# Two convolution outputs from three products instead of four, with operands laid out by phase of the token index

## The chip, the cores and the metric

One core of one Trainium2 chip runs the whole program. The metric is the device time of one execution in microseconds; the kernel before takes 2332 us.

Engine names are the profile's: PE is TensorE's matmuls, PEld its weight loads, DVE VectorE, ACT ScalarE, POOL GpSimd, SP the queue that issues most DMAs.

## The reference, cut to what matters

A layer over 32 graphs of 512 nodes with 256 channels: layer norm and ReLU, then three things that feed a gated unit: a dense graph kernel (with a mask), gates, and a convolution of 17 taps along the tokens. All is fp32.

```python
h = relu(bn1(conv1d(xc, conv1_w, 0)))        # 256 -> 256, one tap
h = bn2(conv1d(h, conv2_w, 8))               # 256 -> 256, 17 taps, padding 8
x_conv = relu(h + xc)
A = exp(-dist) * mask                        # 512 x 512 for each graph
x_nmp = A @ relu(x @ w_msg.T + b_msg)
x_in = concat(x_conv, x_nmp)
# r, z, n from x_in @ w_ih.T and x @ w_hh.T; out = (1 - z) * n + z * x
```

## The kernel before

The 17 taps (padded to 18 = 3 x 3 x 2) are done by a fast algorithm of two levels: at each level three outputs from five products, so 25 products for a group of four batches, with the last factor of two done directly. The code is shortened. A product `m` has weights `w` [2 taps, 2 x 128 input channels, 256] and a moving operand `x2`. Eight such groups give 200 products.

```python
G = 4; U = 57                      # batches a group, blocks of 9 tokens
NU = G * U                         # 228 columns a matmul
cps, acc, gps, tr = ...            # four PSUM pools, two banks each: eight banks
...
w, x2 = WS[m], X2[m].rearrange("p (r v) -> p r v", v=V)
ps = cps.tile([P, N], F32, name="ps_c")[:, :NZ]
for o in range(ND):                                  # ND = 2 halves of the channels
    matmul_sum(ps[:, o * NU : (o + 1) * NU],
        [(w[:, k, i, o * P : (o + 1) * P], x2[:, i * G : (i + 1) * G, k : k + U])
         for k in range(2) for i in range(ND)])      # 2 x 4 matmuls of 228 columns
    yield 1.71                                       # PE time, for the schedule
```

A scheduler in Python writes one instruction list for each engine and mixes several streams in it (convolution, gates, graphs, rows, output); each `yield` gives the PE time of a step. The order of a list is fixed when the program is written. Weights and operands are made ahead:

```python
AHEAD, AHEAD_W = 4, 2
w = cv.tile([P, 2, ND, D], F32, name="w", bufs=3)    # 512 KB, fetched two products ahead
nc.sync.dma_start(w, WD[n])
```

And three users of the transpose pool `tr` (two banks):

```python
def norm_t(b, d):        # input halves d = 0, 1: four transposes, then ACT's ReLU reads them
def factors_t(lane):     # graph factors: one transpose, ACT copies it; four more, ACT copies them
def finish(b, o_sb, c):  # output halves c = 0, 2: four transposes, DVE adds them to the residual
```

## Time and profile before

| | before |
|---|---|
| time | 2332 us |
| PE busy, start-up to 210 us | 133 of 210 us |
| PE busy, convolution 210 to 2153 us | 1919 of 1943 us |
| mean granted TensorE clock | 0.978 |

The lines behind this table stand in the prediction. One line is added here. Columns: stretch in us, its length, then busy time and instructions of PE, PEld, DVE, ACT and POOL, granted clock, DMA share, GB/s.

```profile
210.00:2153.00 1943.00, 1918.91 (x6928) 1231.52 (x6927) 1118.80 (x1741) 541.29 (x758) 312.89 (x185) 1.00 0.43 126
```

In the convolution's stretch PE waits 24 us in all and the clock is full. So the kernel is bound by PE's instruction stream.

### The profile page before, as it was taken

How to read it: one execution, taken by the hardware profiler on the slowest of the kernel's cores; microseconds unless marked ns; L12 is line 12 of the kernel's file. 1: busy time of each engine (PE TensorE's matmuls, PEld its weight loads, DVE VectorE, ACT ScalarE, POOL GpSimd, SP SyncE). 2: the span in 40 equal slices, each digit the busy share in tenths (PEclk: the TensorE clock that was granted, in tenths of full speed). 3: DMA queues.
4: the chain of work that ended last, by engine and by line, in shares of the span. 5: the costliest groups of instructions: out<-in, count | busy, mean ns of one | idle time of the engine just before them, and what ended most of it. 6: DMA issues, size and time to landing. Idle time of an engine off the chain costs nothing.

```text
span 2329.1 us, 21478 instructions
## 1 busy us (share of the span) xinstructions
PE 2212.5 (95%) x7712; PEld 1374.2 (59%) x7712; DVE 1292.6 (56%) x2117; ACT 651.7 (28%) x936; POOL 367.0 (16%) x242
## 2 busy tenths in 40 slices
PE   4768898999999999999999999999999999999998
PEld 2335775665666666666566666656666666666443
DVE  5875766665555655656455655655455535464211
ACT  2442224332324222322224222242313111311211
POOL 1000000111110111122021212212111212222222
PEclk8878999999999999999999999999999999999999
DMA  6665654545444434444434454434333233232121
GB/s 199 180 193 153 181 184 126 149 122 157 144 117 118 126 115 139 136 126 128 112 107 129 131 145 132 113 108 113 135 102 117 82 118 108 100 115 93 63 72 37
DMA packets 388219, 292.58 MB, mean 126 GB/s; under 512 B 280720, under 2 KB 330256, under 8 KB 387472
## 3 DMA queue, kind: packets, MB, share of 16 engines
q1 hardware_dynamic: 370688, 244.53, 37.2%
q10 hardware_dynamic: 17424, 46.67, 5.2%
q8 instruction: 61, 1.00, 0.2%
q14 instruction: 46, 0.38, 0.0%
HBM read 227.69 MB, written 63.44 MB: 125 GB/s over the span
## 4 chain that ended last, share of the span: by engine, by line
PE 87%; DVE 5%; DMA 4%; ACT 2%; issue 1%; POOL 0%; SPq 0%; ACTq 0%; POOLq 0%; DVEq 0%
PE ps_acc L687 42%; PE ps_c L93 24%; PE ps_g L93 8%; PE ps_g L588 8%; PE ps_tr L602 1%; PE ps_g L571 1%; PE ps_tr L254 1%; DMA hd<-hT 1%; PE ps_acc L588 1%; DVE ps_tr L581 1%; DMA w<-wd 1%; PE ps_tr L559 1%; DMA m_sb<-in_adj_dram 1%; DMA nd<-xnmp 1%; ACT w L369 0%
## 5 line engine op out<-in xcount | busy, mean ns | idle before, releaser
L93 PEld LDWEIGHTS ps_c<-x,w 128*128 128x128 f32 x3200 | 602.0, 190 | 142.3 <-issue 120.5
L93 PE MATMUL ps_c<-x,w 128*128 128x228 f32 x3200 | 671.5, 357 | 10.3 <-DMA w<-wd 6.7
L687 PE MATMUL ps_acc<-xconv,wih 128*128 128x512 f32 x768 | 362.1, 594 | 6.2 <-ACT xconv L698 6.2
L687 PE MATMUL ps_acc<-hTb,whh 128*128 128x512 f32 x768 | 357.5, 595 | 4.5 <-DMA hTb<-hd 4.1
L687 PE MATMUL ps_acc<-xnb,wih 128*128 128x512 f32 x768 | 361.2, 593 | 0.0
L724 POOL TENSOR_TENSOR o_sb<-hTb,r 128x512 f32<-128x512 f32 x64 | 101.3, 1583 | 1454.4 <-ACT r L719 1253.3
L718 DVE TENSOR_TENSOR r<-ps_acc,r 128x512 f32<-128x512 f32 x64 | 44.3, 692 | 374.4 <-PE ps_acc L687 374.4
L687 PEld LDWEIGHTS ps_acc<-hTb,whh 128*128 128x128 f32 x768 | 144.9, 190 | 149.3 <-issue 141.6
L687 PEld LDWEIGHTS ps_acc<-xnb,wih 128*128 128x128 f32 x768 | 144.6, 189 | 145.6 <-issue 144.5
L687 PEld LDWEIGHTS ps_acc<-xconv,wih 128*128 128x128 f32 x768 | 143.2, 190 | 144.6 <-issue 132.2
L588 PE MATMUL ps_g<-at,msg 128*128 128x512 f32 x464 | 215.2, 608 | 7.0 <-DVE at L582 7.0
L278 DVE SCALAR_TENSOR_TENSOR x<-x,x 128x471 f32<-128x471 f32 (+1 forms) x184 | 172.8, 939 | 2.6
L275 DVE TENSOR_TENSOR x<-x 128x471 f32<-128x471 f32 x200 | 171.1, 872 | 0.1
L709 DVE SCALAR_TENSOR_TENSOR r<-ps_acc,vec,r 128x512 f32<-128x512 f32 x64 | 48.1, 751 | 220.8 <-PE ps_acc L687 198.8
L588 PEld LDWEIGHTS ps_g<-at,msg 128*128 128x128 f32 x464 | 89.8, 195 | 112.9 <-issue 95.4
L535 DVE TENSOR_TENSOR msg<-ps_g,bmsg 128x256 f32<-128x256 f32 x116 | 48.9, 422 | 170.6 <-PE ps_g L93 170.2
L93 PE MATMUL ps_g<-wmsg,hT 128*128 128x259 f32 x464 | 120.6, 398 | 15.5 <-DVE aug L536 7.8
L715 ACT ACTIVATE z<-ps_acc,brz 128x512 f32<-128x512 f32 x64 | 44.1, 688 | 308.1 <-PE ps_acc L687 300.2
L93 PEld LDWEIGHTS ps_g<-wmsg,hT 128*128 128x128 f32 x464 | 87.7, 196 | 56.2 <-issue 35.9
L725 POOL TENSOR_TENSOR o_sb<-z,o_sb 128x512 f32<-128x512 f32 x64 | 118.1, 1845 | 5.0
L719 ACT ACTIVATE r<-r,vec 128x512 f32<-128x512 f32 x64 | 46.3, 724 | 254.7 <-DVE r L718 254.7
L147 POOL TENSOR_TENSOR rstd<-veps,mhalf 128x4 f32<-128x4 f32 x32 | 37.9, 1184 | 488.2 <-DVE veps L146 488.0
(109 smaller groups left out, 2122.8 us busy)
## 6 DMA issues: line engine op xcount, KB each, us to landing
w<-wd SPq DMA_DIRECT2D x200, 512.0 KB, 3.8
m_sb<-in_adj_dram SPq DMA_DIRECT2D x512, 64.0 KB, 2.4
hd<-hT ACTq DMA_DIRECT2D x32, 512.0 KB, 5.3
nd<-xnmp ACTq DMA_DIRECT2D x64, 256.0 KB, 2.0
hTb<-hd SPq DMA_DIRECT2D x32, 512.0 KB, 4.6
xnb<-nd SPq DMA_DIRECT2D x64, 256.0 KB, 2.8
res<-in_x_dram SPq DMA_DIRECT2D x64, 256.0 KB, 4.0
out_dram<-res SPq DMA_DIRECT2D x64, 256.0 KB, 2.4
```

The lines of the kernel that those rows point to most:

```text
L93: nc.tensor.matmul(ps, lhsT, rhs, start=(i == 0), stop=(i == len(pairs) - 1))
L275: nc.vector.tensor_tensor(dst, get(a), get(b), op=ALU.subtract)
L278: nc.vector.scalar_tensor_tensor(dst, a, -2.0, b, op0=ALU.mult, op1=ALU.add)
L535: nc.vector.tensor_tensor(msg[:, c, :], ps[:, :D], bmsg[:, :D], op=ALU.add)
L588: nc.tensor.matmul(ps, msg[:, c, d * P : (d + 1) * P], at[:, c, :], start=(c == 0), stop=(c == NT - 1))
L687: nc.tensor.matmul(ps, w[:, at + i, cols(o, g)], hT[:, i, :] if k == 0 else x_in[2 * k - 2 + i], start=(k == of[0] and i == 0), stop=(k == ...
L709: nc.vector.scalar_tensor_tensor(r, ps_h, vec[:, _COL["b_hh"] + 2 * ND + o : _COL["b_hh"] + 2 * ND + o + 1], r, op0=ALU.add, op1=ALU.mult,)
L715: nc.scalar.activation(z, ps_z, AF.Sigmoid, bias=brz[:, ND + o : ND + o + 1])
L718: nc.vector.tensor_tensor(r, ps_n, r, op=ALU.add)
L719: nc.scalar.activation(r, r, AF.Tanh, bias=vec[:, _COL["b_ih"] + 2 * ND + o : _COL["b_ih"] + 2 * ND + o + 1],)
L724: nc.gpsimd.tensor_tensor(t, hT[:, o, :], r, op=ALU.subtract)
L725: nc.gpsimd.tensor_tensor(t, z, t, op=ALU.mult)
```

## The change

Two outputs of a two-tap filter need four products directly. With `d0 w0 + d1 w1` and `d1 w0 + d2 w1` they come from three: `(d0 - d1) w0`, `(d2 - d1) w1` and the shared middle `d1 (w0 + w1)`. A block has 18 tokens instead of 9, so a matmul has 4 x 29 = 116 columns: 12 matmuls of 116 columns a product for 8 of 228, 24% fewer columns. For this the operand is laid out by phases of the token index. The core of the diff, with cuts and with comments added:

```diff
-U = 57
+U = 29
+Q = 18
...
+    bps = ctx.enter_context(tc.tile_pool(name="bps", bufs=1, space=PSUM))
-    tr = ctx.enter_context(tc.tile_pool(name="tr", bufs=2, space=PSUM))
+    tr = ctx.enter_context(tc.tile_pool(name="tr", bufs=1, space=PSUM))
...
+    def ends(x2):                      # both differences, on POOL
+        xd = cv.tile([P, 2, RV], F32, name="xd", bufs=2)
+        nc.gpsimd.tensor_tensor(xd, d02, x2[:, 1:2, :].to_broadcast([P, 2, RV]), op=ALU.subtract)
...
-                w = cv.tile([P, 2, ND, D], F32, name="w", bufs=3)
+                w = cv.tile([P, 3, ND, D], F32, name="w", bufs=2)
+                nc.gpsimd.tensor_tensor(w[:, 2], w[:, 0], w[:, 1], op=ALU.add)   # start-up only
...
-    AHEAD, AHEAD_W = 4, 2
+    AHEAD, AHEAD_W = 3, 1
...
+                while len(XD) < min(m + 2, len(X2)):
+                    XD.append(ends(X2[len(XD)]))
+                ps = bps.tile([P, N], F32, name="ps_b")[:, :NH]
+                product(ps, 2, x2)
+                mid = cv.tile([P, NH], F32, name="mid", bufs=2)
+                nc.scalar.activation(mid, ps, AF.Copy)
+                yield 0.88
+                ps = cps.tile([P, N], F32, name="ps_c")[:, :NZ]
+                for k in range(2):
+                    product(ps[:, k * NH : (k + 1) * NH], k, xd[:, k])
+                yield 1.76
...
     def kernel_exp(lane, at):          # four exponentials of a graph
-            pss += [lane.ps(), tr.tile([P, N], F32, name="ps_tr")]
+            lane.ps(), tr.tile([P, N], F32, name="ps_tr"),
+            lane.ps(), bps.tile([P, N], F32, name="ps_b"),
     def masked(lane, b, at, c):
-        ps = tr.tile([P, N], F32, name="ps_tr")
+        ps = lane.ps()
```

So the saving in columns is paid with depth: one bank instead of two for transposes, two buffers instead of three for weights that are half as large again, and two new things a product waits for (its differences and the middle bank). Two smaller cuts: operands are made three products ahead instead of four, and the graphs' messages are sent from the tile `right` of the graph factors instead of a tile of their own.

More of the change, by code (lines that the diff above doesn't have):

```diff
@@ L32 @@
 G = 4
-U = 57
-V = U + 2
-ROW = 9 * V
+U = 29
+V = U + 1
+Q = 18
+LEAD = 9
 ORDER = (3, 0, 4, 2, 1)
@@ L77 @@
     NU = G * U
-    NZ = ND * NU
+    NH = ND * NU
+    NZ = 2 * NH
+    RV = NR * V
     const = ctx.enter_context(tc.tile_pool(name="const", bufs=1))
@@ L126 @@
     wraw = prep.tile([P, ND, 2, 3, 3, D], F32)
-    nc.gpsimd.memset(wraw[:, :, 1, 2, 2, :], 0.0)
+    nc.gpsimd.memset(wraw[:, :, 0, 0, 0, :], 0.0)
     wflat = wraw.rearrange("p i a b c o -> p i (a b c) o")
@@ L160, in bn_affine @@
         return sc, sh
-    h1 = const.tile([P, NR, ROW], F32)
-    nc.gpsimd.memset(h1[:, :, :PAD], 0.0)
-    nc.gpsimd.memset(h1[:, :, PAD + N :], 0.0)
+    h1 = const.tile([P, Q, NR, V], F32)
+    for q, v in ((slice(0, LEAD), slice(0, 1)), (slice(Q - 1, Q), slice(V - 2, V - 1)), (slice(0, Q), slice(V - 1, V))):
+        nc.gpsimd.memset(h1[:, q, :, v], 0.0)
     class Lane:
@@ L263, in conv1 @@
         matmul_sum(ps, [(w1[:, i, o * P : (o + 1) * P], hT[:, i, :]) for i in range(ND)])
-        nc.scalar.activation(
-            h1[:, o * G + b % G, PAD : PAD + N], ps, AF.Relu,
-            bias=bn1_sh[:, o : o + 1], scale=bn1_sc[:, o : o + 1],
-        )
-    def fives(get, new, n):
-        def sub(dst, a, b):
-            nc.vector.tensor_tensor(dst, get(a), get(b), op=ALU.subtract)
+        r, h = o * G + b % G, V - 2
+        blocks = ps[:, : Q * h].rearrange("p (v q) -> p q v", q=Q)
@@ new lines, in conv1, with fives, get @@
+        for dst, src in (
+            (h1[:, LEAD:, r, :h], blocks[:, :LEAD, :]),
+            (h1[:, :LEAD, r, 1 : h + 1], blocks[:, LEAD:, :]),
+            (h1[:, LEAD : LEAD + N - Q * h, r, h], ps[:, Q * h :]),
+        ):
+            nc.scalar.activation(
+                dst, src, AF.Relu, bias=bn1_sh[:, o : o + 1], scale=bn1_sc[:, o : o + 1],
+            )
+    def fives(src, n, new):
+        flat = src.rearrange("p q e -> p (q e)")
+        def get(k, some=n):
+            return src[:, k : k + 3 * some - 2 : 3, :]
+        def sub(dst, a, b):
+            some = n if a < 3 else n - 1
+            nc.vector.tensor_tensor(dst[:, :some, :], get(a, some), get(b, some), op=ALU.subtract)
+            if a > 2:
+                at = [src[:, 3 * n - 3 + b, :], flat[:, (b - 3) * RV + 1 : (b - 2) * RV + 1]]
+                nc.vector.tensor_tensor(
+                    dst[:, some, :], flat[:, (a - 3) * RV + 1 : (a - 2) * RV + 1], at[b > 2],
+                    op=ALU.subtract,
+                )
@@ L277, in less2 @@
         def less2(dst, a, b):
             nc.vector.scalar_tensor_tensor(dst, a, -2.0, b, op0=ALU.mult, op1=ALU.add)
+        size = n * RV
         d1 = new()
-        sub(d1[:, :n], 3, 1)
-        yield d1, n
+        sub(d1, 3, 1)
+        yield d1, size
         for a, b in ((2, 0), (4, 2)):
             t = new()
-            sub(t[:, :n], a, b)
-            yield None, n
+            sub(t, a, b)
+            yield None, size
             if b == 0:
-                less2(t[:, :n], t[:, :n], d1[:, :n])
+                less2(t, t, d1)
@@ L289, in fives @@
             else:
-                less2(t[:, :n], d1[:, :n], t[:, :n])
-            yield t, n
+                less2(t, d1, t)
+            yield t, size
         f2 = new()
-        sub(f2[:, :n], 3, 2)
-        yield None, n
+        sub(f2, 3, 2)
+        yield None, size
         t = new()
-        sub(t[:, :n], 2, 1)
-        yield None, n
-        less2(t[:, :n], t[:, :n], f2[:, :n])
-        yield t, n
-        less2(f2[:, :n], get(1), f2[:, :n])
-        yield f2, n
-    N1, N2 = NR * ROW // 3 - 1, NR * V - 1
+        sub(t, 2, 1)
@@ L305, in operands @@
+        yield None, size
+        less2(t, t, f2)
+        yield t, size
+        less2(f2, get(1), f2)
+        yield f2, size
     def operands():
-        h1f = h1.rearrange("p r t -> p (r t)")
         for x1, size in fives(
-            lambda k: h1f[:, k : k + 3 * N1 - 2 : 3],
-            lambda: cv.tile([P, NR * ROW // 3], F32, name="x1", bufs=3),
-            N1,
+            h1.rearrange("p q r v -> p q (r v)"), 6,
+            lambda: cv.tile([P, 6, RV], F32, name="x1", bufs=3),
         ):
@@ L313, in operands @@
             yield None, size
-            if x1 is None:
-                continue
-            yield from fives(
-                lambda k: x1[:, k : k + 3 * N2 - 2 : 3],
-                lambda: cv.tile([P, NR * V], F32, name="x2", bufs=7),
-                N2,
-            )
-    WD = [dram.tile([P, 2, ND, D], F32, name=f"wd{n}") for n in range(25)]
+            if x1 is not None:
+                yield from fives(x1, 2, lambda: cv.tile([P, 2, RV], F32, name="x2", bufs=6))
+    def ends(x2):
+        xd = cv.tile([P, 2, RV], F32, name="xd", bufs=2)
+        d0 = x2[:, 0, :]
+        d02 = bass.AP(d0.tensor, d0.offset, [d0.ap[0], (1, 2), (1, RV)])
+        nc.gpsimd.tensor_tensor(
+            xd, d02, x2[:, 1:2, :].to_broadcast([P, 2, RV]), op=ALU.subtract
+        )
+        return xd
@@ L324, in taps_of @@
+    WD = [dram.tile([P, 3, ND, D], F32, name=f"wd{n}") for n in range(25)]
     def taps_of(get, new, inplace):
@@ L344, in weights_first @@
         nonlocal made_w
+        made = None
         outer = [
@@ L366, in weights_first @@
             for j2 in ORDER:
-                w = cv.tile([P, 2, ND, D], F32, name="w", bufs=3)
+                w = cv.tile([P, 3, ND, D], F32, name="w", bufs=2)
                 for i in range(ND):
                     nc.scalar.activation(
-                        w[:, :, i, :], next(inner[i]), AF.Copy, scale=GSCALE[j1] * GSCALE[j2]
+                        w[:, :2, i, :], next(inner[i]), AF.Copy, scale=GSCALE[j1] * GSCALE[j2]
                     )
                     yield
-                nc.scalar.dma_start(WD[made_w], w)
-                made_w += 1
+                nc.gpsimd.tensor_tensor(w[:, 2], w[:, 0], w[:, 1], op=ALU.add)
+                if made is not None:
+                    nc.scalar.dma_start(WD[made_w], made)
+                    made_w += 1
+                made = w
+        nc.scalar.dma_start(WD[made_w], made)
+        made_w += 1
     def weights_again():
         for n in range(25):
-            w = cv.tile([P, 2, ND, D], F32, name="w", bufs=3)
+            w = cv.tile([P, 3, ND, D], F32, name="w", bufs=2)
             nc.sync.dma_start(w, WD[n])
@@ L388, in summed @@
     def summed(g):
-        y = yf = None
+        y = None
         def add(dst, a, b, op=ALU.add, size=3 * NZ):
@@ L397, in copy, with more, both @@
             SUMS.append((lambda: nc.scalar.activation(dst, src, AF.Copy, scale=scale), 500))
-        def twice(dst, a, b):
+        def more(dst, a, k, b, op=ALU.add):
             SUMS.append((
-                lambda: nc.vector.scalar_tensor_tensor(dst, a, 2.0, b, op0=ALU.mult, op1=ALU.add),
+                lambda: nc.vector.scalar_tensor_tensor(dst, a, k, b, op0=ALU.mult, op1=op),
                 NZ,
             ))
+        def both(dst, got):
+            ps, mid = got
+            nc.vector.tensor_tensor(
+                dst.rearrange("p (h n) -> p h n", h=2), ps.rearrange("p (h n) -> p h n", h=2),
+                mid[:, None, :].to_broadcast([P, 2, NH]), op=ALU.add,
+            )
@@ L405, in summed @@
         for j1 in ORDER:
-            ps = yield
+            got = yield
             n3 = cv.tile([P, NZ], F32, name="n", bufs=3)
-            nc.scalar.activation(n3, ps, AF.Copy)
-            ps = yield
+            both(n3, got)
+            got = yield
             sum_all()
             z = cv.tile([P, 3, NZ], F32, name="z")
-            ends = z[:, 0:3:2, :]
-            zf = z.rearrange("p e n -> p (e n)")
-            nc.vector.tensor_tensor(z[:, 0, :], ps, n3, op=ALU.add)
-            ps = yield
@@ L416, in summed @@
-            nc.vector.scalar_tensor_tensor(z[:, 2, :], n3, 4.0, ps, op0=ALU.mult, op1=ALU.add)
-            ps = yield
-            n2 = cv.tile([P, NZ], F32, name="n", bufs=3)
-            nc.scalar.activation(n2, ps, AF.Copy)
-            ps = yield
-            s = cv.tile([P, NZ], F32, name="s")
-            nc.vector.tensor_tensor(s, ps, n2, op=ALU.add)
-            nc.vector.tensor_tensor(n2, ps, n2, op=ALU.subtract)
-            add(ends, ends, s[:, None, :].to_broadcast([P, 2, NZ]), size=2 * NZ)
@@ L425, in summed @@
-            twice(z[:, 1, :], n3, n2)
+            zends = z[:, 0:3:2, :]
+            both(z[:, 0, :], got)
+            add(z[:, 0, :], z[:, 0, :], n3, size=NZ)
+            got = yield
+            both(z[:, 2, :], got)
+            more(z[:, 2, :], n3, 4.0, z[:, 2, :])
+            got = yield
+            n2 = cv.tile([P, NZ], F32, name="n", bufs=3)
+            both(n2, got)
+            got = yield
+            n1 = cv.tile([P, NZ], F32, name="n1")
+            both(n1, got)
+            add(n2, n1, n2, ALU.subtract, size=NZ)
@@ L426, in summed @@
+            more(n1, n1, 2.0, n2, ALU.subtract)
+            add(zends, zends, n1[:, None, :].to_broadcast([P, 2, NZ]), size=2 * NZ)
+            more(z[:, 1, :], n3, 2.0, n2)
             if j1 == 3:
@@ L428, in summed @@
                 y = late.tile([P, 3, 3, NZ], F32, name="y")
-                yf = y.rearrange("p f e n -> p f (e n)")
-                copy(yf[:, 0], zf, 1.0)
-                copy(yf[:, 1], zf, 2.0)
-                copy(yf[:, 2], zf, 4.0)
+                copy(y[:, :, 0], z, 1.0)
+                copy(y[:, :, 1], z, 2.0)
+                copy(y[:, :, 2], z, 4.0)
             elif j1 in (0, 4):
-                add(yf[:, j1 // 2], yf[:, j1 // 2], zf)
+                add(y[:, :, j1 // 2], y[:, :, j1 // 2], z)
             else:
-                for e in range(3):
-                    add(yf[:, e], yf[:, e], zf, ALU.subtract if (e, j1) == (1, 2) else ALU.add)
+                for f in range(3):
+                    add(y[:, :, f], y[:, :, f], z, ALU.subtract if (f, j1) == (1, 2) else ALU.add)
         EVAC.extend((y, b, o) for b in range(g * G, (g + 1) * G) for o in range(ND))
@@ L450, in evacuate @@
         if o == 0:
-            XC[b] = late.tile([P, ND, 9 * U], F32, name="xconv", bufs=4)
+            XC[b] = late.tile([P, ND, Q * U], F32, name="xconv", bufs=4)
         c = o * NU + b % G * U
         nc.scalar.activation(
-            XC[b][:, o, :].rearrange("p (u e f) -> p f e u", e=3, f=3), y[:, :, :, c : c + U],
+            XC[b][:, o, :].rearrange("p (u h k) -> p k h u", h=2, k=9),
+            y.rearrange("p e f (h n) -> p (e f) h n", h=2)[:, :, :, c : c + U],
             AF.Identity, bias=bn2_sh[:, o : o + 1], scale=bn2_sc[:, o : o + 1],
@@ L458, in evacuate @@
             evacuated.add(b)
-    AHEAD, AHEAD_W = 4, 2
+    AHEAD, AHEAD_W = 3, 1
     XC, evacuated = {}, set()
-    X2, WS = [], []
+    X2, XD, WS = [], [], []
     at_product = 0
@@ L481, in operand_some @@
                 freed = len(X2) // 25
-        return 1.5 * size
+        return size
     def convolution():
@@ L503, in convolution, with product @@
                         yield lambda: made > g
-                w, x2 = WS[m], X2[m].rearrange("p (r v) -> p r v", v=V)
-                ps = cps.tile([P, N], F32, name="ps_c")[:, :NZ]
-                for o in range(ND):
-                    matmul_sum(
-                        ps[:, o * NU : (o + 1) * NU].rearrange("p (b u) -> p b u", u=U),
-                        [
-                            (w[:, k, i, o * P : (o + 1) * P], x2[:, i * G : (i + 1) * G, k : k + U])
-                            for k in range(2)
-                            for i in range(ND)
-                        ],
-                    )
-                    if o == 0 and done is not None:
-                        sums.send(done)
-                    yield 1.71
-                WS[m] = X2[m] = None
-                done = ps
+                while len(XD) < min(m + 2, len(X2)):
+                    XD.append(ends(X2[len(XD)]))
+                w, xd = WS[m], XD[m].rearrange("p h (r v) -> p h r v", v=V)
+                x2 = X2[m][:, 1, :].rearrange("p (r v) -> p r v", v=V)
+                def product(ps, k, moving):
+                    for o in range(ND):
+                        matmul_sum(
+                            ps[:, o * NU : (o + 1) * NU].rearrange("p (b u) -> p b u", u=U),
+                            [
+                                (w[:, k, i, o * P : (o + 1) * P], moving[:, i * G : (i + 1) * G, :U])
+                                for i in range(ND)
+                            ],
+                        )
+                ps = bps.tile([P, N], F32, name="ps_b")[:, :NH]
+                product(ps, 2, x2)
+                mid = cv.tile([P, NH], F32, name="mid", bufs=2)
+                nc.scalar.activation(mid, ps, AF.Copy)
+                if done is not None:
+                    sums.send(done)
+                yield 0.88
+                ps = cps.tile([P, N], F32, name="ps_c")[:, :NZ]
+                for k in range(2):
+                    product(ps[:, k * NH : (k + 1) * NH], k, xd[:, k])
+                yield 1.76
+                WS[m] = X2[m] = XD[m] = None
+                done = ps, mid
             sums.send(done)
@@ L564, in kernel_exp @@
     def kernel_exp(lane, at):
-        pss = []
-        for c in range(NT // 2):
-            pss += [lane.ps(), tr.tile([P, N], F32, name="ps_tr")]
+        pss = [
+            lane.ps(), tr.tile([P, N], F32, name="ps_tr"),
+            lane.ps(), bps.tile([P, N], F32, name="ps_b"),
+        ]
         for c in range(NT):
@@ L592, in gather @@
                 yield 1.73
-        xnmp = front.tile([P, N], F32, name="xnmp", bufs=1)
-        nc.scalar.activation(xnmp, ps, AF.Copy)
-        nc.scalar.dma_start(ND_[b, d], xnmp)
+        nc.scalar.activation(lane.right, ps, AF.Copy)
+        nc.scalar.dma_start(ND_[b, d], lane.right)
         yield 1.73
@@ L848 @@
         for c in range(ND):
-            nc.sync.dma_start(wflat[:, c, k0:k1, :], conv2_w[:, c, k0:k1, :])
+            nc.sync.dma_start(wflat[:, c, k0 + 1 : k1 + 1, :], conv2_w[:, c, k0:k1, :])
     streams = {
@@ L858 @@
         "other graphs": (all_graphs(lanes[1]), 54.0, -1.27),
-        "conv": (convolution(), 85.5, 0.0),
+        "conv": (convolution(), 66.0, 0.0),
         "gates": (all_gates(), 125.0, 1.1),
```

## The prediction

> **What bounds the kernel now.** I read the page's shares and slices first, then busy time by stretch, then the timeline of a few microseconds.
>
> ```profile
> PE 2212.5 (95%) x7712; PEld 1374.2 (59%) x7712; DVE 1292.6 (56%) x2117; ACT 651.7 (28%) x936; POOL 367.0 (16%) x242
> ...
> PE   4768898999999999999999999999999999999998
> ...
> L93 PEld LDWEIGHTS ps_c<-x,w 128*128 128x128 f32 x3200 | 602.0, 190 | 142.3 <-issue 120.5
> L93 PE MATMUL ps_c<-x,w 128*128 128x228 f32 x3200 | 671.5, 357 | 10.3 <-DMA w<-wd 6.7
> ```
>
> ```profile
> 0.00:210.00 210.00, 132.90 (x380) 69.56 (x381) 138.68 (x334) 76.12 (x136) 13.83 (x27) 0.82 0.62 182
> 210.00:400.00 190.00, 174.58 (x745) 130.66 (x744) 129.98 (x227) 55.32 (x85) 4.14 (x3) 0.96 0.57 169
> 400.00:2150.00 1750.00, 1741.33 (x6170) 1098.14 (x6169) 988.82 (x1515) 485.97 (x674) 306.89 (x181) 1.00 0.41 121
> ```
>
> The second fence gives stretches: length, busy time of PE, weight loads, DVE, ACT and POOL, then clock and DMA. The first 210 us are start-up; the convolution runs from 210 to 2153 us, and from 400 us PE is busy 1741 of 1750 us. There every saved PE microsecond counts in full, and so does every new PE wait[...].
>
> What a matmul costs is its spacing, not its recorded duration:
>
> ```profile
> 1005.11 1.70 PE L93 MATMUL ps_c<-x,w 128*128 128x228 f32 x8
> 1008.37 1.70 PE L93 MATMUL ps_c<-x,w 128*128 128x228 f32 x8
> ...
> 1037.23 1.04 PE L602 MATMUL ps_tr<-ident,o_sb 128*128 128x128 f32 x8
> 1038.10 1.88 PE L687 MATMUL ps_acc<-xconv,wih 128*128 128x512 f32 x4
> ```
>
> Eight in 1.70 us with a last one of 0.36 us are (1.70 - 0.36) / 7 = 0.192 us apart; for 512 columns (1.88 - 0.59) / 3 = 0.43; for 128 columns (1.04 - 0.27) / 7 = 0.110. So spacing is about 0.83 ns a column plus 2.5 ns. Each fp32 product of the source is two such instructions.
>
> [...] between two fp32 weight loads of the convolution the shortest distance is 108 ns (17 times) and 110 (44 times), although each is recorded with 190. [...] behind the 5.2 us gap at 242 us and the 4.1 us gap at 380 us the clock was 0.5 for 6.8 us each. [...] Here a 1368-element sum took 1.58 us alone, 2.65 beside a POOL instruction. [...]
>
> **The change part by part.**
> *Matmuls.* Before, 25 x 8 products x 8 matmuls x 2 = 3200 instructions of 228 columns at 192.5 ns: 616 us. After, 12 matmuls a product: 4800 instructions of 4 x 29 = 116 columns. Columns alone would give 99 ns, but the next weights need 108 to 110. I choose 109: 523 us. Saved: 93 us, not the 141 us of the columns.
> *The transpose bank (tr), from two buffers to one.* This I take as the main cost. Masks no longer use it, but three pairs of users follow each other:
>
> ```profile
> 1037.23 1.04 PE L602 MATMUL ps_tr<-ident,o_sb 128*128 128x128 f32 x8
> ...
> 1038.52 0.68 DVE L606 TENSOR_TENSOR res<-ps_tr,res 128x512 f32<-128x512 f32 x1
> ...
> 1039.82 0.69 DVE L606 TENSOR_TENSOR res<-ps_tr,res 128x512 f32<-128x512 f32 x1
> ```
>
> ```profile
> 1053.41 0.27 PE L555 MATMUL ps_tr<-ident,augl 128*128 128x128 f32 x1
> 1053.41 0.47 PEld L559 LDWEIGHTS ps_tr<-ident,augr 128*128 128x128 f32 x4 [0.29 <-issue]
> ...
> 1053.72 0.28 ACT L556 ACTIVATE left<-ps_tr 128x128 f32<-128x128 f32 x1 [1.08 <-PE ps_tr L555]
> ```
>
> The eight output transposes ran in one go; with one buffer the last four wait until DVE has read the first four (here to 1039.20 instead of 1037.67). The graph factors' four transposes wait for ACT's copy (here to 1054.0 instead of 1053.52). I went through all such pairs of the trace and added the time from when the second began to when the reader of the first ended, plus 0.06 us: output 32 pairs, 43.5 us; factors 32 pairs, 34.5 us; the two halves of a normalised input 26 pairs, 57.7 us. After 210 us that is about 95 us. Of the 41 us before it I count 12, since PE idles 77 us there anyway.
> *The new bank (bps).* The middle product shares it with the fourth exponential of a graph. In 13 of 32 graphs the next convolution product began before that exponential had ended: 20 us in all.
> *The differences on POOL.* 200 instructions of 480 elements, which the next product needs. POOL takes 1.27 us for 512 elements undisturbed, 1.6 to 1.8 in the mean of its rows: about 1.6 each, 320 us more on POOL, which is no bound. But they are made only one product ahead and stand behind the three POOL steps of a gate mix:
>
> ```profile
> 1764.81 9.62 PE L93 MATMUL ps_c<-x,w 128*128 128x228 f32 x48
> ...
> 1766.54 1.78 POOL L724 TENSOR_TENSOR o_sb<-hTb,r 128x512 f32<-128x512 f32 x1 [19.99 <-ACT r L719]
> ...
> 1768.40 2.54 POOL L725 TENSOR_TENSOR o_sb<-z,o_sb 128x512 f32<-128x512 f32 x1
> ...
> 1771.02 1.72 POOL L726 TENSOR_TENSOR o_sb<-r,o_sb 128x512 f32<-128x512 f32 x1
> ```
>
> Three products run back to back right after a mix; POOL is free at 1772.7, the next difference is there at 1774.4, and the second product wants it near 1768.8. Over all products, with 1.7 us for a difference, 22 would wait, 70 us; without those that the wait before them removes, 50.
> *Third weight matrix.* 768 KB instead of 512: 3.8 us to landing becomes perhaps 5.7 (estimate by size), fetched one product ahead rather than two. Only runs of three or more products outrun that; 13 such cases, about 15 us.
> *DVE and ACT.* Operands get dense: 471 elements with a step of three take 0.80 us, dense about 0.64; but three of five differences are split. Net about -36 us. Partial sums grow from six DVE instructions (4.4 us) to eleven (five of 0.64, five of 0.63, one of 1.12: 7.4 us) for each of 40 outer steps: +121 us. Collisions with the doubled POOL work: +70. DVE goes from 1293 to about 1450 us, 62%: longer queues, no bound. ACT: +32 us for the middle copies less the two it loses, +50 for three conv1 pieces instead of one.
> *Gone.* PE's waits for the masks' transposes, about 10 us. *Clock.* Perhaps ten new gaps over 3 us[...]: 15 us.
> *Sum.* Costs 95 + 12 + 20 + 50 + 15 + 15 = 207 us. They were taken one by one; a stall lets the other engines catch up, so I count three quarters, 155. 2333 - 93 - 10 + 155 = 2385 us.
>
> **The rivals.** First: the matmuls win. If output, factors and input pay only their shortest waits after 210 us (32 x 0.94 + 26 x 0.54 + 20 x 0.85 = 61 us) and nothing else stalls, the time is 2333 - 93 - 10 + 61 = 2291. For it speaks that conv work often lies between the users; against it that the output pairs are always adjacent. If in addition weights hid behind 116 columns at 99 ns, 48 us less: about 2245. Second: all waits in full, with POOL contention and DVE queues making them longer: 2333 - 103 + 207 and more, 2440 to 2470. The 5 to 7 us that POOL lags behind a mix speak for it. Third: weight loads take their recorded 190 ns each and become the bound: 4800 x 0.19 = 912 us, near 2630. Against it: matmuls of 128 columns start 109 ns apart while such loads run.
>
> **Range and chances.** The certain part, -93 and +61, lands close to even; the rest is only upward. I predict 2385 us, 2310 to 2455 eight times in ten. Faster by over 2% (below 2286) needs nearly no new wait: 0.11. Within 2%: 0.36. Slower (above 2379): 0.53.
>
> **What would show it.** The changed profile should have 4800 convolution matmuls about 109 ns apart; PE busy near 88 to 91%, with new idle time before output, factor and input transposes ended by DVE and ACT, and before convolution matmuls ended by POOL; the clock below 1.00 in stretches after 400 us; DVE near 62%, POOL near 30%. I am wrong if the spacing is 99 or 190, if PE stays at 98% after 400 us, or if the transposes do not wait.

## The result, and the profile after

The changed kernel takes **2692.6 us** (2689.0 to 2695.1, 4 runs) against 2332.1 us. The ratio is 1.1544, 95% interval 1.1524 to 1.1564. All ratios here are the mean time of one kernel's fast runs over that of the other's of the same rounds, so they are not quite the ratio of the medians quoted. The output of the kernel is correct. The direction was the likelier one of the prediction, but the loss is 360 us where 52 were predicted.

First the page of the changed kernel: shares, PE's busy tenths in 40 slices, and the granted clock in tenths.

```profile
PE 2267.2 (84%) x9312; PEld 1385.3 (52%) x9312; DVE 1471.7 (55%) x2461; ACT 712.1 (27%) x1184; POOL 642.0 (24%) x468
...
PE   5537786888878899989899888998998899899998
...
PEclk8767898988989999989999999999999999999999
```

Then the stretches of start-up, convolution and tail, with the columns told above:

```profile
0.00:258.40 258.40, 138.97 (x380) 73.09 (x381) 147.37 (x333) 80.61 (x152) 50.42 (x54) 0.76 0.57 173
258.40:2503.70 2245.30, 1964.80 (x8529) 1239.08 (x8528) 1288.98 (x2084) 597.19 (x990) 552.97 (x384) 0.94 0.43 132
2503.70:2687.00 183.30, 163.48 (x407) 73.14 (x406) 35.39 (x44) 34.32 (x42) 38.60 (x30) 0.97 0.17 55
```

The reader is to see two things. PE idles 280 us in the convolution's stretch (2245.3 - 1964.8), not 24. And PE's busy time there did not fall by the saving: it rose by 46 us, with a clock of 0.94 instead of 1.00. Where PE waited over the whole span, as the view of waits tells it (total, times, longest; `ps_b` is the bank of the middle product, `ps_c` one of the two differences' products, `ps_tr` the transpose bank):

```profile
PE ps_b L98 <- DMA w<-wd: 97.5, 32, 10.6
PE ps_tr L616 <- ACT left L613: 62.8, 32, 15.3
PE ps_tr L260 <- ACT hT L261: 50.1, 24, 12.2
PE ps_c L98 <- POOL xd L345: 35.8, 18, 6.7
PE ps_tr L659 <- DVE res L663: 31.6, 32, 3.4
PE ps_b L98 <- ACT at L634: 22.5, 9, 6.6
```

Every one of these is a buffer that the change made scarcer or a dependence that it added: weights, the transpose bank three times, the differences, the middle bank. But the waits at the transpose bank are only in part the convolution's: of their 144.5 us, 76 lie there (24.1, 20.5 and 31.6) and 68 in start-up; the others lie in the convolution.

The clock is read best in a timeline of PE (start, duration, instruction, count, idle time before and what ended it):

```profile
1476.89 1.04 PE L98 MATMUL ps_b<-x,w 128*128 128x116 f32 x8
1477.77 1.95 PE L98 MATMUL ps_c<-xd,w 128*128 128x116 f32 x16
...
1485.00 2.02 PE L98 MATMUL ps_b<-x,w 128*128 128x116 f32 x8 [3.50 <-DMA w<-wd]
1486.82 3.62 PE L98 MATMUL ps_c<-xd,w 128*128 128x116 f32 x16
```

The same eight and sixteen matmuls take 1.04 and 1.95 us, and right after a 3.5 us gap 2.02 and 3.62 us. This gap cost its length, and then the granted clock was 0.5 from 1484.2 us for 6.8 us and PE's work took nearly twice as long.

The books, from the matmul records and the clock records of the two traces. The convolution is counted from its first to its last matmul's start, the tail from there to PE's last matmul; the granted clock is recorded in windows, and each is 1.0 or 0.5 (12 windows of 0.5 in the trace of before, 57 in that of the changed kernel):

| part | before | after | difference |
|---|---|---|---|
| start-up, to the first convolution matmul | 210.0 | 258.4 | +48 |
| convolution: PE idle | 24.1 | 280.5 | +256 |
| convolution: PE busy | 1919.1 | 1964.8 | +46 |
| of it half clock: half of PE's busy time in such windows (11.9 and 202.4 us) | 6 | 101 | +95 |
| of it convolution matmuls: 3200 x 0.1925 and 4800 x 0.1117 us | 616 | 536 | -80 |
| of it the rest (not worked out further) | | | +31 |
| tail, to PE's last matmul | 171.7 | 179.4 | +8 |

### The profile page after: what moved, and what is told of

Its sections match the earlier page's. It is cut to its first block, busy times and chain, and to the rows that moved or that the text cites. A ratio compares the mean times of both kernels' runs of the same rounds, so it can differ in the third digit from the quotient of the medians.

```text
span 2687.0 us, 25967 instructions
## 1 busy us (share of the span) xinstructions
PE 2267.2 (84%) x9312; PEld 1385.3 (52%) x9312; DVE 1471.7 (55%) x2461; ACT 712.1 (27%) x1184; POOL 642.0 (24%) x468
## 5 line engine op out<-in xcount | busy, mean ns | idle before, releaser
L98 PEld LDWEIGHTS ps_c<-xd,w 128*128 128x128 f32 x3200 | 412.5, 205 | 88.7 <-issue 46.5
L98 PE MATMUL ps_c<-xd,w 128*128 128x116 f32 x3200 | 422.4, 289 | 35.8 <-POOL xd L345 35.8
L345 POOL TENSOR_TENSOR xd<-x 128x480 f32<-128x480 f32 x200 | 283.2, 1423 | 686.7 <-PE ps_c L98 296.2
L744 PE MATMUL ps_acc<-hTb,whh 128*128 128x512 f32 x768 | 371.7, 616 | 3.7 <-ACT r L763 3.7
L98 PE MATMUL ps_b<-x,w 128*128 128x116 f32 x1600 | 238.6, 297 | 152.0 <-DMA w<-wd 97.5
L98 PEld LDWEIGHTS ps_b<-x,w 128*128 128x128 f32 x1600 | 223.6, 210 | 215.2 <-issue 151.9
L567 ACT ACTIVATE mid<-ps_b 128x232 f32<-128x232 f32 x200 | 72.7, 363 | 423.4 <-PE ps_b L98 396.7
L304 DVE SCALAR_TENSOR_TENSOR x<-x,x 128x480 f32<-128x480 f32 (+1 forms) x184 | 169.4, 920 | 2.3
L295 DVE TENSOR_TENSOR x<-x 128x240 f32<-128x240 f32 (+1 forms) x200 | 132.5, 662 | 0.9
L443 DVE TENSOR_TENSOR n<-ps_c,mid 128x464 f32<-128x464 f32 x120 | 76.0, 633 | 88.6 <-PE ps_c L98 87.4
```

Source lines behind the costliest of these rows:

```text
L98: nc.tensor.matmul(ps, lhsT, rhs, start=(i == 0), stop=(i == len(pairs) - 1))
L295: nc.vector.tensor_tensor(dst[:, :some, :], get(a, some), get(b, some), op=ALU.subtract)
L304: nc.vector.scalar_tensor_tensor(dst, a, -2.0, b, op0=ALU.mult, op1=ALU.add)
L345: nc.gpsimd.tensor_tensor(xd, d02, x2[:, 1:2, :].to_broadcast([P, 2, RV]), op=ALU.subtract)
L443: nc.vector.tensor_tensor(dst.rearrange("p (h n) -> p h n", h=2), ps.rearrange("p (h n) -> p h n", h=2), mid[:, None, :].to_broadcast([P, ...
L567: nc.scalar.activation(mid, ps, AF.Copy)
```

## The experiments

Fourteen kernels ran. Names with a_ are the changed kernel with edits, names with b_ the kernel before with edits; the fourteenth, a_split, ran once and is told last. Some variants were found to deadlock before they were run: a third weight buffer whose room was taken from the partial sums or from the middle copies, and a schedule that lets the operands run still further ahead.

| run | edit | time, us | ratio to before | PE idle in the convolution, us | mean clock |
|---|---|---|---|---|---|
| changed kernel | | 2692.6 | 1.1544 | 280 | 0.925 |
| a_wq | weights fetched from ACT's queue | 2681.4 | 1.1492 | 259 | 0.925 |
| a_xd | differences on DVE | 2655.2 | 1.1378 | 258 | 0.935 |
| a_tr | successive users of the transpose bank spread | 2661.8 | 1.1415 | 267 | 0.921 |
| a_w3 | three weight buffers, two ahead | 2639.8 | 1.1323 | 269 | 0.930 |
| a_all | a_wq, a_xd, a_tr, exponential order | 2548.3 | 1.0927 | 175 | 0.937 |
| a_all3 | a_w3, a_xd, a_tr, exponential order | 2492.0 | 1.0689 | 162 | 0.938 |
| a_cps | and one pool of three banks | 2469.7 | 1.0583 | 144 | 0.941 |
| a_best | and start-up banks, operands earlier | 2437.5 | 1.0454 | 133 | 0.951 |
| a_light | and less DVE work (wrong result) | 2412.0 | 1.0340 | 117 | 0.952 |
| a_poolbest | a_best, differences on POOL again | 2498.5 | 1.0714 | 171 | 0.942 |
| b_tr | before, one transpose bank | 2441.6 | 1.0473 | 97 | 0.974 |
| b_w1 | before, two weight buffers, one ahead | 2368.6 | 1.0153 | 50 | 0.972 |
| b_both | before, both cuts | 2479.8 | 1.0628 | 120 | 0.969 |

### The depth alone, on the kernel before

This is the direct test of the main theory: take the depth away and leave the four products.

```diff
# b_tr
-    tr = ... bufs=2
+    tr = ... bufs=1
+    bps = ... bufs=1                 # for the fourth exponential only
     def masked: ps = tr.tile(...)    ->  ps = lane.ps()
# b_w1
-    w = ... bufs=3;  AHEAD_W = 2
+    w = ... bufs=2;  AHEAD_W = 1
```

> The kernel before with only the transpose bank cut to one buffer, the masks moved off it and the fourth exponential on a bank of its own. My theory: PE gets the waits before output, factor and input transposes that I added up from its trace, 95 us after start-up and some in it, and loses clock by them: slower by 110 to 190 us. Rival (waits of this kind are absorbed, since what PE waits for would have been waited for later anyway): slower by less than 60 us.

> The kernel before with only the weight buffers cut from three to two and the fetch one product ahead. My theory: with 512 KB instead of 768 and longer products the waits for weights are smaller than in the changed kernel, 30 to 60 us, and the time rises by 40 to 90 us. Rival (only the larger fetch makes it late): slower by less than 20 us.

> The kernel before with both cuts, one transpose bank and two weight buffers. They cost 110 and 37 us singly. My theory (short gaps cost their length and no clock): they add, 2450 to 2500, with a mean clock of 0.96 to 0.975. Rival (gaps together bring the clock down, as in the changed kernel): above 2520 and a clock below 0.95.

Measured: 2441.6 us, 2368.6 us and together 2479.8 us against 2332 us, so +110, +37 and +148. They add. (At the threshold of 2% the second alone would count as the same as before; its interval, 1.3 to 1.75% slower, is clear of zero. It stayed just under the 40 to 90 us expected, and the first is at the lower edge of its 110 to 190.) PE's waits of the run with one transpose bank:

```profile
PE ps_tr L255 <- ACT hT L256: 51.8, 24, 13.6
PE ps_tr L603 <- DVE res L607: 36.0, 32, 4.4
PE ps_tr L560 <- ACT left L557: 32.2, 32, 7.5
```

These are 120 us for the three pairs; the prediction had added up 43.5, 34.5 and 57.7 us for output, factors and input from the trace of before. After start-up they are 81 us (36.0, 18.3 and 26.6), for about 95 predicted, and PE's idle time in the convolution rose by 73. Of the run with two weight buffers:

```profile
PE ps_c L93 <- DMA w<-wd: 38.0, 22, 6.5
```

So a single buffer less costs 37 us even with the old 512 KB fetch. And the clock of the run with one transpose bank stays nearly full after start-up:

```profile
PE 2239.3 (92%) x7712; PEld 1376.9 (56%) x7712; DVE 1296.2 (53%) x2117; ACT 654.7 (27%) x936; POOL 365.8 (15%) x242
...
PEclk8778999999999999999999999999999999999999
```

What follows: waits of this kind are not absorbed elsewhere in a kernel whose PE hardly idles; in the convolution 81 us of waits became 73 us of idle time. The rival of absorption falls. But both cuts together explain 148 us, and little of that is clock: half of PE's busy time in half-clock windows of the convolution is 13 us with one transpose bank and 27 us with both cuts, against 6 before and 101 in the changed kernel. The changed kernel must have something beyond them.

### What a gap does to the clock

This was not a run but a count over 13 traces (the kernel before, the changed kernel and eleven runs: all but the split run, a_light and a_poolbest): every gap of PE over 0.4 us after 280 us, and whether a half-clock window began between its start and 3.6 us after its end.

| gap, us | gaps | followed by half clock |
|---|---|---|
| 0.4 to 1 | 460 | 7% |
| 1 to 1.5 | 258 | 6% |
| 1.5 to 2 | 114 | 30% |
| 2 to 2.5 | 92 | 66% |
| 2.5 to 3.5 | 104 | 85% |
| 3.5 to 5 | 82 | 96% |
| over 5 | 86 | 100% |

In these traces a gap up to 1.5 us mostly cost its length alone (half clock followed 6 to 7% of them); over 2.5 us it nearly always brought a window of half clock (85 to 100%). The kernel before has 2 gaps over 2.5 us after 280 us, the run with one transpose bank 6, the changed kernel 38. That is why lost depth in the kernel before cost 148 us but only 21 us of clock, while the changed kernel loses 95 us in the convolution. The long gaps of the changed kernel are mostly those before `ps_b` and `ps_c`, ended by the weights, the differences and the operands.

The traces also show when a gap of 2 us does it and when not. In the traces of the two kernels all half-clock windows (12 and 57) begin on one grid with steps of 3.41 us. In the changed kernel's convolution a step at full clock with PE busy under 45% was followed by half clock 37 of 39 times, one with 45 to 55% 5 of 15 times, one with more 1 of 527 times; so it counted here how a gap fell on the grid. (45, 55 and 90% are the bounds chosen for this count.) And half clock ended after 41 of the 41 steps with PE busy over 90%, but after only 2 of the 36 others: with new waits it lasted longer. (PE's ends are modelled, so these shares are near ones.)

This bears on the rival named for a_wq below, that small matmuls and not gaps lower the clock. At 116 columns it falls: 42 of the 43 windows of the changed kernel began behind a step that was at most 55% busy. At the 58 columns of a_split (one run), which the table leaves out, it holds in part: 18 of 35 windows began behind a step over 55% busy, and they sum to 556 us, for 263 in the changed kernel, with only 11 gaps over 2.5 us.

### The weights: queue or depth

```diff
# a_wq
-            nc.sync.dma_start(w, WD[n])
+            nc.scalar.dma_start(w, WD[n])
# a_w3 (room from single buffers for the rows' input and small tiles)
-    w = ... bufs=2;  AHEAD_W = 1
+    w = ... bufs=3;  AHEAD_W = 2
```

> The changed kernel, with the convolution's weights fetched from ACT's queue instead of SP's, where twelve mask loads can stand ahead of them. My theory (PE waits on thinned buffers, each wait also costing half clock after it): PE's 97 us of waits for weights shrink to under 30 us and the time falls by 80 to 130 us, to about 2580. Rival (the fetch of 768 KB one product ahead is itself too late, whatever the queue): waits stay above 70 us and the time within 30 us of 2693. Rival on the clock (small matmuls, not gaps, lower it): mean clock stays at 0.925.

> The changed kernel with a third buffer for the weights and the fetch two products ahead again (the room comes from single buffers for the rows' input and some small tiles). My theory now: the depth of the prefetch, not the queue, makes the 97 us of waits for weights, so these fall below 20 us; since the runs before showed that PE then meets the next late thing sooner, the time falls by 40 to 90 us, to about 2630. Rival (768 KB a product is too much for the DMA engines as such): waits stay above 60 us and the time within 25 us of 2693.

The first theory was the queue, because of places like this one in the changed kernel (the second and third line are SP issuing DMAs, not the engine working):

```profile
761.84 1.04 PE L98 MATMUL ps_b<-x,w 128*128 128x116 f32 x8
...
762.36 4.40 SPq L198 DMA_DIRECT2D m_sb<-in_adj_dram  x8
...
766.85 0.43 SPq L413 DMA_DIRECT2D w<-wd  x1
...
772.55 2.02 PE L98 MATMUL ps_b<-x,w 128*128 128x116 f32 x8 [7.89 <-DMA w<-wd]
```

Eight mask loads stand ahead of the fetch, which is issued 5 us after the previous product began. But off that queue the waits only fell to 86.9 us and the time to 2681 us (from 2693): a miss, and the queue theory falls. (The mean clock stayed at 0.925, the sign of the rival on the clock, but with the waits still there this decides nothing.) With the third buffer they all but vanish:

```profile
PE ps_c L98 <- POOL xd L345: 78.8, 28, 6.7
...
PE ps_b L98 <- DMA w<-wd: 6.2, 2, 5.6
```

The time falls by 53 us to 2640, but most of that is not the convolution's. What both runs say together: the fetch stands in the instruction list at the place of the previous product, and both queues that were tried got there at about that product's time. Of the 49 products of the changed kernel that began within 0.4 us of their weights' landing, 40 had their fetch issued only after the previous product had begun; on ACT's queue it was 37 of 43. In 34 of the 49 the previous product had not followed closely on the one before it, so two products in a row are enough. The landing takes 4.6 us at the median, and the next product often comes after less. One product ahead is a distance in the program, not a time. Start-up also got shorter, 231 us to the first convolution matmul instead of 258, with a third buffer for the weights that are made there; ACT had waited 51.4 us for their stores. That is 28 us, over half of the gain; PE's idle time in the convolution fell by only 12.

The first line of the fence is the other lesson: freed of the weights, PE waits 78.8 us for the differences where it had waited 35.8, and 53.5 us instead of 31.6 before the output's transposes.

### The transpose bank and the differences, one at a time

```diff
# a_tr: other work between successive users of the one bank
     finish(b, unfinished[b], c)
-    yield 0.55
+    yield 0.55, 4.0                  # ready again 4 us later
     norm_t(b, d):    yield 0.55, 2.0 * d  ->  yield 0.55, 4.0 - 2.0 * d
     factors_t(lane): a yield of 0.14, 3.0 between its two parts
# a_xd
-        nc.gpsimd.tensor_tensor(xd, ...)
+        nc.vector.tensor_tensor(xd, ...)
```

> The changed kernel, still with one transpose bank, but other work scheduled between its successive users (output halves, graph factors, input halves). My theory: of the 144 us of PE waits before those transposes over 100 go and the time falls by 110 to 170 us, to about 2550. Rival (the waits come from ACT and DVE being late, not from adjacency): waits fall by less than 50 us and the time by less than 60.

> The changed kernel, with the differences of the operands on DVE instead of POOL. My theory: PE's 36 us of waits for the differences go, DVE gets 200 x 0.65 = 130 us more work, and the time falls by 20 to 50 us. Rival (the DVE queue is the real delay, so anything put on it comes back as waits): no gain, or slower by up to 60 us, with more PE waits for DVE.

Spreading worked as an edit and missed as a saving: 2661.8 us, 31 us less, not 110 to 170. PE's waits in that run:

```profile
PE ps_b L98 <- DMA w<-wd: 120.1, 38, 8.9
...
PE ps_b L98 <- DVE x L304: 33.2, 8, 8.1
...
PE ps_tr L617 <- ACT left L613: 4.7, 4, 2.1
```

The factors' wait is down from 62.8 to 4.7 us, but the one for weights is up from 97.5 to 120.1 and the one for operands from 11.7 to 33.2. PE simply arrives sooner at the next thing that is late. The edit had also less to give than was reckoned: 68 of the 144 us lay in start-up, which became only 2 us shorter. Of the convolution's 76 us under 10 are left. The differences on DVE gave 37 us, within the 20 to 50 expected: PE idles 22 us less, and half of its busy time at half clock fell from 101 to 84 us.

### All together

> The three edits of the runs before together, and the exponential that holds the product's bank evacuated first. My theory: they add, PE's idle time in the convolution falls from 280 to under 80 us, the mean clock rises above 0.96, and the time is 2360 to 2430. Rival (the form with three products is slow by itself: more sums on DVE, weight loads at 112 ns): the time stays above 2550 with PE waiting elsewhere.

> The third weight buffer with the differences on DVE, the transposes spread and the exponential's order changed. My theory: most named waits are gone together, nothing is left for them to move to, and the time falls below 2470 us, about 2440, with a mean clock of 0.95 or more. Rival (waits just move to DVE and start-up): above 2520 us.

a_all reads the four exponentials in the order 3, 1, 0, 2, so that the middle product's bank is free first. It takes 2548.3 us: 144 us less than the changed kernel, where its three main edits gave 11, 37 and 31 one by one. With the third weight buffer in place of the other queue (a_all3) it is 201 us less. So the edits give more together than one by one. That the waits lie in series on PE, so that a single repair only moves PE on to the next one, fits the single runs but was not tested apart from the fourth edit: the exponentials' order never ran alone. PE's waits for exponentials before `ps_b` fell from 22.5 to 12.7 us in a_all, which is too little for the other 65 us. Both expectations were too hopeful: 2360 to 2430 for the first and below 2470 for the second, which with 2492 lies between theory and rival (above 2520). PE still waits elsewhere.

```diff
# a_cps: the middle product and the fourth exponential share the outer products' pool
-    cps = ... bufs=2;  bps = ... bufs=1
+    cps = ... bufs=3
     # and the exponentials in the order 1, 3, 0, 2
# a_best: start-up's transposes use those banks too; more operand work for DVE a step
-    pace(pe, 2.0 if at_product == 0 else 0.8 if at_product < 25 else 0.45)
+    pace(pe, 2.0 if at_product == 0 else 1.1 if at_product < 25 else 0.58)
```

> The kernel with the third weight buffer, differences on DVE and spread transposes, and now the middle product, the outer products and the fourth exponential in one pool of three banks in place of one bank for the middle product and two for the outer. My theory: the waits of about 31 us for exponentials and 12 us for the middle copies, most of them single gaps of 2 to 8 us, go, and the time falls by 30 to 70 us from 2492. Rival (the outer products then wait for DVE's sums instead): within 20 us of 2492.

> The same, with the transposes of start-up in the banks that the convolution does not use yet, and DVE's operand work let run further ahead by the schedule's pace. My theory: start-up shortens by 10 to 25 us and PE's waits for operands (over 50 us, mostly in the first group) fall by half: 2360 to 2420, still not below the kernel before. Rival (DVE or the order of the schedule is the real bound in start-up and first group): within 25 us of the run before.

2469.7 and 2437.5 us: 22 us (less than the 30 to 70 expected) and 32 us more, the second ending above the 2360 to 2420 expected. That is 255 us of the 360 taken back, with the same arithmetic.

```profile
PE 2193.2 (90%) x9312; PEld 1339.5 (55%) x9312; DVE 1520.4 (62%) x2661; ACT 711.0 (29%) x1186; POOL 354.2 (15%) x268
```

PE's busy time is now 19 us below the 2212.5 of the kernel before, but it still idles 133 us in the convolution and loses 50 us there to half clock (6 before).

### Why the repaired kernel is still slower

> The repaired kernel with a wrong result on purpose: the large running sums of the outputs add 24 elements instead of 1392, 64 instructions of 1.6 us fewer for DVE, about 95 us, all else the same. Theory (DVE's longer queue makes PE's remaining waits): the time falls by 40 to 100 us, to 2340 to 2400. Rival (the waits come from the order of the schedule and thin buffers, and DVE is only the last link): it falls by less than 25 us.

> The repaired kernel with the differences back on POOL. Theory (POOL, with the gate mixes ahead in its queue, hands them over late): slower by 15 to 50 us than 2437. Rival (DVE's load is what counts): faster by 10 to 50 us.

```diff
# a_light: the running sums add 24 elements instead of 1392 (wrong result on purpose)
-    add(y[:, :, f], y[:, :, f], z, ...)
+    add(y[:, :, f, :8], y[:, :, f, :8], z[:, :, :8], ...)
```

With 92 us of DVE's busy time taken away, the time falls by 25 us, to 2412.0: between the two expectations (40 to 100, or less than 25). DVE's load is a part of the remainder, not most of it. With the differences back on POOL it rises by 61 us, to 2498.5, more than the 15 to 50 expected, because they stand behind the gate mixes again (the three POOL instructions that end a gate's work). In 15 of these 18 waits the difference came right behind a mix's last step:

```profile
PE ps_c L97 <- POOL xd L351: 54.1, 18, 6.7
```

So POOL's place in line costs more than DVE's extra work. What makes the rest, about 105 us over the kernel before, was not settled: by the books of a_best PE idles 109 us more in the convolution, spread over many waits, start-up takes 18 us more, and PE's busy time in the convolution is 19 us less, with 44 us more lost to half clock in it. No version that was tried beats the kernel before.

### The floor under a small matmul

```diff
# a_split: each matmul cut in two halves of 58 columns, same weights
-    ps[:, o * NU : (o + 1) * NU] += w[...] @ moving[:, four batches, :U]
+    for h in range(2): ps[:, half h] += w[...] @ moving[:, two batches of half h, :U]
```

> The changed kernel with each convolution matmul cut in two of 58 columns under the same weights, so twice as many instructions and weight loads for the same columns. My theory (the load of the next weights, 108 to 112 ns, is the floor): they stand 112 ns apart as before, 9600 x 0.112 = 1075 us instead of 536, and the time rises to 3100 or more. Rival (the distance follows the columns, 0.83 ns each plus some overhead): about 65 ns apart and a time below 2800.

One look, 3226 us (one run, state unknown). Two lines of its timeline:

```profile
1513.32 3.67 PE L98 MATMUL ps_c<-xd,w 128*128 128x58 f32 x32
...
1521.20 1.89 PE L98 MATMUL ps_b<-x,w 128*128 128x58 f32 x16
```

A matmul of 58 columns is recorded with about 0.21 us, so 32 of them stand (3.67 - 0.21) / 31 = 0.112 us apart. In the whole trace the middle half of the distances is 111 to 112 ns, as it is with 116 columns. The distance in a stream does not follow the columns, and the rival of 65 ns falls. A fixed cost of every matmul would give the same distance, but the trace speaks against it: in 227 places the first two matmuls behind other work stand 50 to 55 ns apart, and the spacing of 0.83 ns a column plus 2.5 ns, read from the trace of before, gives 51 ns for 58 columns; in 213 places of the changed kernel they stand 98 to 102 ns apart, where it gives 99 ns for 116 columns. So these pairs stand as close as their columns. The shortest distance between two weight loads of the convolution is 108 ns in the traces of the kernel before and of the changed kernel. The time of 3226 us agrees with the 3100 or more expected partly by luck: more half clock and less idle time than in the changed kernel also went into it.

## Why the prediction was wrong, point by point

*Matmuls, saved 93 us.* Right in mechanism: in a stream the distance was not that of the columns (111 to 112 ns with 116 and with 58 columns), and the weight loads of the changed kernel mostly start 111 to 112 ns apart too. It is 111.7 ns in the mean, not 109: 80 us saved at full clock.

*The transpose bank, 95 us after start-up and 12 in it.* Right in mechanism, a little high after start-up: 81 us of waits in b_tr and 76 in the changed kernel. That b_tr as a whole cost 110 us, near 95 + 12, is in part luck, since its start-up, its tail and its busy time in the convolution grew too (by 9, 6 and 22 us). In start-up these waits are 68 us in the changed kernel, for the 41 added up.

*The middle bank, 20 us.* Right: 22.5 us of waits for exponentials.

*The differences, 50 us.* Right in mechanism, a little high: 35.8 us of waits. The 37 us gained when they moved are not the same sum: part is clock, and DVE made PE wait for 18 us of them. DVE near 1450 us and POOL near 690 were predicted; 1472 and 642 were measured.

*The third weight matrix, 15 us: failed.* The step said that only runs of three or more products outrun the fetch. The fetch was often issued only after the product before had begun (40 of the 49 cases above), and two products in a row are enough: 97.5 us of waits, although the landing took 4.6 us and not the 5.7 estimated. With the third buffer these waits fell to 6.2 us.

*The clock, 15 us: failed, the largest error.* "Perhaps ten new gaps over 3 us" was a guess, and 15 us for ten of them went against the prediction's own two examples: a PE that is busy throughout 6.8 us at half clock loses 3.4 us. There are 27 gaps over 3 us and 38 over 2.5, already from 2 us on most gaps were followed by half clock (66% of those of 2 to 2.5 us; the trace of before has one such window itself, at 1132.6 us behind a gap of 2.4 us), and the 43 windows in the convolution last 6.1 us in the mean. Cost 95 us, in addition to idle time.

*Start-up, 12 us: failed.* 48 us. The store of the weights behind two buffers was not looked at; 28 of the 48 came back with a third buffer. The transposes' waits there were larger than added up (68 us); what they cost in time was not separated.

*The discount to three quarters: failed.* It was argued that a stall lets the others catch up. The two cuts add without discount (110 + 37 = 147, measured 148). Repairs go the other way: in a_w3 and a_tr one gave back much less than its own wait, since other things were late.

The terms of the first sum were 207 us of cost; the books come to 438: idle 256 + clock 95 + start-up 48 + tail and rest 39, against 80 saved (358 net). Of the rest, 31 us of busy time stay unexplained. The rival that was closest, all waits in full and more at 2440 to 2470, had the right mechanism and also lacked the clock. The sign of a profile gone wrong that the prediction named, PE at 88 to 91% and a clock below 1.00, was there, only stronger: 84% and 0.94.

## What to carry to other kernels

In a kernel whose critical engine never waits, buffers are what the speed is made of: before giving up a bank or a prefetch slot, go through the trace and add up, for each pair of successive users, how long the second would have waited for the reader of the first. Ask of each new wait how long a single one is: here waits of one microsecond mostly cost PE their sum alone (half clock followed 6 to 7% of the gaps up to 1.5 us), while those over 2.5 us nearly always cost it the clock too (85 to 100%). And with a weight load for every matmul, 58 columns took the same 112 ns as 116 here, so an algorithm like this one, which trades columns for instructions, has to be priced by instructions.
